# Layer-norm statistics of the last three pairs placed two rounds later, and the Silu table load placed behind the last softmax exponent

## The chip, the core and the metric

The kernel runs on one core of a Trainium2 chip. The core has five engines with an instruction stream each, executed in order: TensorE (PE in the profile; PEld is its weight load), VectorE (DVE), ScalarE (ACT), GpSimd (POOL) and SyncE (SP). They wait for each other and for DMA transfers through semaphores. SP and POOL each issue DMA transfers in this kernel. The metric is the device time of one execution in microseconds (us); lower is better. The time before is 755.1 us, the median of three runs (752.46, 755.1 and 756.65).

## The reference, cut to what matters

Input `x` is 32 sequences of 56 tokens with 256 features; `ctx` is 32 contexts of 1500 rows by 256 with a mask. There are four residual steps, each on a layer norm of what came before:

```python
x = x + xattn0(layernorm(x), ctx)          # decayed scan over the context, its mean projected, layer norm
x = x + ffn0(layernorm(x))                 # 16 experts, the best 6 of each token, hidden width 176
x = x + xattn1(layernorm(x), ctx, mask)    # softmax(q k / 16) over unmasked rows, times the rows
x = x + ffn1(layernorm(x))                 # 2 experts, the better one of each token, hidden width 1024
# an expert: (silu(h @ w_gate.T) * (h @ w_up.T)) @ w_down.T, weighted by its gate's softmax
```

`layernorm` subtracts the mean over the 256 features and divides by the root of the variance plus 1e-5. In `xattn1` queries are the rows of the norm, and keys and values are both the context rows. The mask leaves a run of rows at the end of each context, so the kernel reads a window of 384 rows per context (and has a branch at its end for inputs to which this doesn't apply; it is not taken here).

## The kernel before, in words

All arithmetic is in fp32. Two sequences together are a *pair*: 2 x 64 partitions, of which 2 x 56 hold tokens, so there are 16 pairs (`NP`), and the residual stream stays in SBUF as `xr[:, p, :]`, 128 partitions by 256 features for pair `p`.

There are four stages, each with its tile pools, so each begins as the one before ends:

1. The context scan (`xattn0`), the norm, the first gate and a sort of the tokens by expert.
2. The first expert stage: 99 blocks of 128 sorted rows. Each block's rows are gathered by POOL, multiplied with the weights of its expert, and its result is written to a DRAM buffer `ys0`. As blocks are done, the six results of each token are fetched again and added to `xr`. For pairs 0 to 12 (`NS` = 13) this is done inside the stage, by plain gathers and adds on DVE, and so are their statistics (mean and variance of `xr[:, p, :]`, function `stats_into`, lines 862 to 865: one bn_stats, one aggregate).
3. The attention (`xattn1`), lines 1107 to 1386.
4. The second expert stage (`expert_blocks` from line 1387 on): 15 blocks of four units, each unit gate and up products (L785), Silu on ACT (L791), a product on DVE (L795), two transposes (L803), a copy (L805) and the down product (L812). It begins with the rows that were sorted first.

In stages 2 to 4 a manual schedule is in force: every engine executes its instructions in the order in which the program text emits them. So the place of a line in the text is its place in the queue of its engine.

The attention is a loop over rounds `p` = 0 to 16 (line 1327). One round holds work of several pairs, one step apart:

- at `p == NR - 6` = 4 and `p == NP - 5` = 11, the roots of statistics that are ready (`roots_of`, lines 882 to 887: Ln and Exp on ACT, L189 and L190, then L885 on DVE); at round 11 those of pairs 13, 14, 15
- the normalised row block of pair `p + 2` (`query_rows`, ACT, L890), which reads these roots
- the root of pair `p - 2`'s last norm (ACT, L189 and L190)
- the scores of pair `p` (TensorE, L1133 and L1139) and the attended rows of pair `p - 1` (TensorE, L1174)
- the row maximum of pair `p` (DVE, L1147) and the softmax exponent (ACT, L1152)
- the last norm and gate of pair `p - 2` (DVE, L1200, L1207)
- attended rows times the softmax inverse plus residual, of pair `p - 1` (`sort_rows`, DVE, L1190), into a *payload* tile `pay`, and its statistics (L183, L184); then, in the round of pair 7's payload, the issue of the second expert stage's weights on SP (`load_w1`, L1101 and L1105)
- for pair `p + 2` the transposes of the query (TensorE L902, copied by ACT, L904) and of the window (TensorE L913, copied by DVE and ACT in turns, L916)
- the transposes of pair `p`'s probabilities (TensorE L1166, copied by ACT, L1167)
- for each four pairs the choice of expert, the rank and the place of each token (`sort_four`, `sort_rank`, `sort_place`), and four scatters of the payloads into sorted order by POOL (L1258)
- three of the 18 accumulating gathers of pairs 13 to 15 (`added`, POOL, L1318): each adds one of six results from `ys0` to `xr[:, p, :]` by DMA, so all stand in POOL's queue ahead of what the later rounds give it, and a pair's next gather waits for its last one. POOL runs behind the other engines here: it issues the last of them at 555.10 us, in the time of round 8
- at the end of round 8 (`p == NP - 8`), the statistics of pairs 13, 14 and 15 (`stats_into`, DVE, L864 and L865)
- in round 11 the order of the sorted blocks (`order_of_blocks`, one TensorE product, L1274, and ten DVE instructions from L1275 to L1291), in round 12 the first three gathers of sorted rows (L1305), and in round 15 the transposes and the copy of the first of them (L195, L197).

Round 16 holds only what is left of pairs 14 and 15.

Buffers matter in two places. The pool of payload tiles has nine buffers (line 1111), used in turn, so from pair 9 on a payload is written to a buffer that an earlier one's scatter must have left. And the PSUM pool `at_x` has four banks for the five transposes of a round (one of the query, four of the window), so the window's last transpose needs the bank that the query's copy (L904) empties. The attended rows have one PSUM bank: the next attend waits until DVE has read the one before (L1190).

ACT's functions come in table sets, one of which is active at a time. The attention opens with an explicit request for the set that holds Ln and Exp (L1121). The set for Silu is not asked for in the text: its load stands directly ahead of the first Silu of stage 4 (L791).

Of the kernel before, what the change touches and what calls it, by code (L numbers as in the profile page):

```python
# [22 lines left out]
NP = B // 2  # L23
# [35 lines left out]
def xattn_ffn_kernel(  # L59
# [23 lines left out]
    V, A, PE, G = nc.vector, nc.scalar, nc.tensor, nc.gpsimd  # L83
# [783 lines left out]
    def roots_by_steps(mv, n=1):  # L867

        m, v, y, r = (mv[..., i] if n > 1 else mv[:, i : i + 1] for i in range(4))
        i = y.bitcast(I32)  # L870
        yield lambda: V.tensor_scalar(v, v, EPS, None, ALU.add)  # L871
        yield lambda: V.tensor_scalar(i, v.bitcast(I32), 1, None, ALU.logical_shift_right)
        yield lambda: V.tensor_scalar(i, i, -1.0, float(0x5F3759DF), ALU.mult, ALU.add)
        c = small.tile([P, NP], F32, tag="nw", name="c")[:, 0:n]
        for _ in range(3):
            yield lambda: V.tensor_tensor(c, y, y, ALU.mult)
            yield lambda: V.tensor_tensor(c, c, v, ALU.mult)
            yield lambda: V.tensor_scalar(c, c, -0.5, 1.5, ALU.mult, ALU.add)
            yield lambda: V.tensor_tensor(y, y, c, ALU.mult)
        yield lambda: V.scalar_tensor_tensor(r, m, -1.0, y, ALU.mult, ALU.mult)  # L880

    def roots_of(a, b):

        inverse_root(mvq[:, a:b, 2], mvq[:, a:b, 1])
        V.scalar_tensor_tensor(  # L885
            mvq[:, a:b, 3], mvq[:, a:b, 0], -1.0, mvq[:, a:b, 2], ALU.mult, ALU.mult
        )
# [4 lines left out]
    def query_rows(p, pool):  # L892

        xn = pool.tile([P, D], F32, tag="xq_n", bufs=2, name="xn")
        normed(xn, xr[:, p, :], mvq[:, p])
        return xn

    def queries(p, pool, ps, tag, xn):

        tp = ps.tile([P, 512], F32, tag=tag, name="tp")  # L900
        for k in range(KD):
            PE.transpose(tp[:, k * P : (k + 1) * P], xn[:, k * P : (k + 1) * P], ident)  # L902
        xqs[p] = pool.tile([P, KD, P], F32, tag="xq", bufs=2, name="xq")
        A.activation(  # L904
            xqs[p].rearrange("p k c -> p (k c)"), tp[:, 0:D], AF.Copy, scale=ISC
        )
# [191 lines left out]
    def load_w1():  # L1098
        for m, w in ((0, wg1), (1, wu1)):
            for k in range(KD):  # L1100
                nc.sync.dma_start(  # L1101
                    out=w1_sb[:, :, (2 * k + m) * fq : (2 * k + m + 1) * fq],
                    in_=w[:, k, :].rearrange("p (e f) -> p e f", f=fq),
                )
        nc.sync.dma_start(  # L1105
            out=w1_sb[:, :, 2 * KD * fq : W1].rearrange("p e (c d) -> p e c d", d=D),
            in_=wd1.rearrange("p (e c) d -> p e c d", c=2),
        )
# [3 lines left out]
    with tc.manual_schedule(  # L1112
# [13 lines left out]
        def scores(p):  # L1126

            sps = psc.tile([P, 512], F32, tag="sp", name="sp")
            cT, xq = cTs.pop(p), xqs.pop(p)
            halves = [(h, slice(64 * h, 64 * h + 64)) for h in range(2)]  # L1130
            for h, r in halves:
                b = 2 * p + h
                PE.matmul(  # L1133
                    sps[r, 0:WIN], lhsT=pick[:, b : b + 1].to_broadcast([P, 64]),
                    rhs=terms.rearrange("b (q j) -> b j q", j=JW), start=True, stop=False,
                )
            for k in range(KD):
                for h, r in halves:
                    PE.matmul(  # L1139
                        sps[r, 0:WIN], lhsT=xq[:, k, r], rhs=cT[:, h, k, :],  # L1140
                        start=False, stop=(k == KD - 1),
                    )
            return sps

        def highest(sps):
            nb = small.tile([P, 4], F32, tag="nb", name="nb")
            V.tensor_reduce(nb[:, 0:1], sps[:, 0:WIN], AX.X, ALU.max, negate=True)  # L1147
            return nb

        def softmax(sps, nb):  # L1150
            sc = at.tile([P, WIN], F32, tag="sc", name="sc")
            A.activation(sc, sps[:, 0:WIN], AF.Exp, bias=nb[:, 0:1], accum_out=nb[:, 1:2])  # L1152
            return sc

        def inverse(nb):
            V.reciprocal(nb[:, 1:2], nb[:, 1:2])

            V.scalar_tensor_tensor(
                nb[:, 2:3], nb[:, 0:1], 0.5 * BIG, nb[:, 1:2], ALU.is_lt, ALU.mult
            )  # L1160
# [9 lines left out]
        def attend(p, pT):  # L1170
            op = po.tile([P, 512], F32, tag="op", name="op")
            for j in range(JW):
                for h in range(2):
                    PE.matmul(  # L1174
                        op[64 * h : 64 * h + 64, 0:D],
                        lhsT=pT[:, j, 64 * h : 64 * h + 64], rhs=window(p, h)[:, j, :],
                        start=(j == 0), stop=(j == JW - 1),
                    )
            return op
# [8 lines left out]
        def sort_rows(p, op, nb):  # L1188
            pay[p] = payp.tile([P, WP], F32, tag="pay", name="pay")
            V.scalar_tensor_tensor(  # L1190
                pay[p][:, D : 2 * D], op[:, 0:D], nb[:, 2:3], xr[:, p, :], ALU.mult, ALU.add
            )
            G.tensor_copy(pay[p][:, WP - 1 : WP], toks[:, p : p + 1])
            return stats(pay[p][:, D : 2 * D])

        def sort_root(mv):
            inverse_root(mv[:, 2:3], mv[:, 1:2])

        def sort_norm(p, mv):
            V.tensor_scalar(  # L1200
                pay[p][:, 0:D], pay[p][:, D : 2 * D], mv[:, 0:1], mv[:, 2:3],
                ALU.subtract, ALU.mult,
            )

        def sort_gate(p):
            gx = so.tile([P, D], F32, tag="gx", name="gx")
            V.scalar_tensor_tensor(  # L1207
                gx, pay[p][:, 0:D], 1.0, gd, ALU.mult, ALU.mult, accum_out=dd[:, p : p + 1]
            )
# [103 lines left out]
        def apart():  # L1313

            G.memset(gap, 0.0)
# [11 lines left out]
        for p in range(NP + 1):  # L1327
            if p == NR - 6:
                roots_of(NR, NS)
            if p == NP - 5:  # L1330
                roots_of(NS, NP)

            if p + 2 < NP:
                xn = query_rows(p + 2, at)
            if p - 2 in mvs:
                if p < NP:
                    sort_root(mvs[p - 2])
                else:
                    for step in roots_by_steps(mvs[p - 2]):
                        step()  # L1340
            if p < NP:
                sps = scores(p)
            if held:
                op = attend(held[0], held[1])
            if p < NP:
                nb = highest(sps)
                sc = softmax(sps, nb)
            if p - 2 in mvs:
                sort_norm(p - 2, mvs.pop(p - 2))
                sort_gate(p - 2)  # L1350
            if held:
                mvs[held[0]] = sort_rows(held[0], op, held[2])
                if held[0] == 7:
                    load_w1()
                held = None
            if p + 2 < NP:
                queries(p + 2, at, px, "x", xn)
                cTs[p + 2] = at.tile([P, 2, KD, WIN], F32, tag="cT", name="cT")
                for i in range(2 * KD):
                    turn(p + 2, i, px, "x", V.tensor_copy if i % 2 == 0 else A.copy)  # L1360
                    if i == 0:
                        inverse(nb)
            elif p < NP:
                inverse(nb)
            if p < NP:
                held = (p, turned(sc), nb)
            if four:
                sort_place(*four[0], sort_rank(four.pop()[1], ppt, "pt"))
            if 0 <= p - 2 and (p - 2) % GP == GP - 1:
                o = p - 2 - GP + 1  # L1370
                four.append((o, sort_four(o)))
            for q in range(NP - NS):
                if todo:
                    added(*todo.pop(0))
            if p == NP - 8:
                for q in range(NS, NP):
                    stats_into(mvq[:, q], xr[:, q, :])
            if p == 11:
                order_of_blocks()
            if p == 12:  # L1380
                for i in range(NY1):
                    apart()
                    rows_of1(i, payp, "pay")
            if p == NP - 1:
                xT1 = turned_rows(so, px, "x", xb1[0][:, 0:D])
# [229 lines left out]
```

## Time and profile before

The profiled execution took 789.92 us, and its span from first to last instruction is 788.0 us.

| stage | us from start | length | PE busy | DVE busy | ACT busy | granted PE clock | DMA share | GB/s |
|---|---|---|---|---|---|---|---|---|
| context scan, sort | 0 to 214 | 214.0 | 157.73 | 149.11 | 56.14 | 0.87 | 0.87 | 303 |
| first experts | 214 to 513 | 299.0 | 268.72 | 131.94 | 105.52 | 0.97 | 0.54 | 161 |
| attention | 513 to 602.42 | 89.42 | 80.53 | 62.68 | 50.90 | 0.96 | 0.72 | 209 |
| second experts | 602.42 to 788 | 185.58 | 172.99 | 60.86 | 29.69 | 0.99 | 0.11 | 34 |

All times are microseconds. "Busy" is the time in which an engine had an instruction in execution; matmuls are pipelined, so a busy TensorE isn't TensorE at its peak. The granted clock is a share of full speed. The DMA share is the mean busy share of the core's 16 DMA engines. In the timeline lines that follow, the first number is the start from the span's beginning, the second the time taken; then come engine, line of the kernel, operation, and the tile written and those read (`out<-in`), and in brackets the idle time of that engine just before the instruction with what ended it. The chain of waits is followed back from the last instruction: at each step to what released it, or to the instruction before it on its engine. What ended a wait is inferred from semaphore events.

### The profile page before, as it was taken

What the parts mean: (1) busy time and instruction counts of PE and PEld (TensorE: products, weight loads), DVE (VectorE), ACT (ScalarE), POOL (GpSimd) and SP (SyncE); (2) the same over time, 40 slices, a digit from 0 to 9 for tenths busy, and PEclk for the clock granted to TensorE, in tenths of its full rate; (3) what the DMA queues carried; (4) which work ended last, traced back from release to release, by engine and by line L of the source; (5) the groups of instructions that cost most, each with busy time, mean ns of one, the idle gap of its engine ahead of it and who ended that gap; (6) DMA issues with size and microseconds to landing.
All of it is one profiled execution on the core that took longest, in us unless ns stands there. A gap on an engine that the chain in (4) does not pass through costs nothing.

```text
span 788.0 us, 13691 instructions
## 1 busy us (share of the span) xinstructions
PE 680.0 (86%) x4147; PEld 447.8 (57%) x4147; DVE 404.6 (51%) x1386; ACT 242.2 (31%) x716; POOL 354.0 (45%) x444
## 2 busy tenths in 40 slices
PE   3477988887789889889899889899797999999995
PEld 3334545554467667556667566666464566666663
DVE  3568677788436436234444345667587333233321
ACT  0123233333134333333333333366463111111110
POOL 5355566643343465556656665457542411122110
PEclk9879799997699999899999999999899999999998
DMA  8969899999258976334434444387961200110100
GB/s 260 351 258 376 321 346 381 359 340 238 72 161 269 329 224 197 107 106 137 133 114 131 133 133 134 107 251 181 257 224 48 94 13 21 41 35 27 33 27 18
DMA packets 71426, 137.69 MB, mean 175 GB/s; under 512 B 7859, under 2 KB 43844, under 8 KB 71348
## 3 DMA queue, kind: packets, MB, share of 16 engines
q1 hardware_dynamic: 56612, 100.84, 37.4%
q0 software_dynamic: 14736, 35.90, 16.9%
q8 instruction: 39, 0.64, 0.3%
q14 instruction: 39, 0.32, 0.1%
HBM read 110.07 MB, written 27.29 MB: 174 GB/s over the span
## 4 chain that ended last, share of the span: by engine, by line
PE 72%; DVE 7%; DMA 5%; ACT 3%; issue 3%; POOL 3%; another core or an unknown queue 1%; POOLq 0%; ACTq 0%; DVEq 0%
PE gu L785 29%; PE y L812 18%; PE acc L325 6%; PE tp L803 4%; PE tp L195 4%; DMA xr<-ys,back 4%; ACT xT L197 2%; PE owned L593 1%; POOL xr L1318 1%; PE bp L467 1%; PE lp L505 1%; POOL xn L491 1%; PE sT L459 1%; PE tp L913 1%
## 5 line engine op out<-in xcount | busy, mean ns | idle before, releaser
L785 PE MATMUL gu<-w_sb,xT 128*128 x396 | 142.1, 482 | 23.9 <-ACT xT L197 19.7
L943 POOL DMA_INDIRECT xb<-xn,idx x99 | 96.6, 976 | 103.1 <-PE tp L195 52.1
L791 ACT ACTIVATE sg<-gu 128x176 f32<-128x176 f32 (+1 forms) x159 | 54.4, 342 | 239.5 <-PE gu L785 206.9
L797 DVE SCALAR_TENSOR_TENSOR hs<-sg,wgt,gu 128x176 f32<-128x176 f32 x99 | 39.3, 397 | 158.4 <-ACT sg L791 136.3
L785 PE MATMUL gu<-ring,xT 128*128 x240 | 112.9, 593 | 0.5 <-issue 0.5
L785 PEld LDWEIGHTS gu<-w_sb,xT 128*128 128x128 f32 x396 | 73.6, 194 | 61.9 <-ACT xT L197 27.5
L812 PE MATMUL y<-w_sb,hT 88*128 x396 | 103.6, 384 | 0.8 <-ACT yb L951 0.8
L856 POOL DMA_INDIRECT g<-ys,early x78 | 74.0, 949 | 33.5 <-issue 18.0
L795 DVE TENSOR_TENSOR hs<-sg,gu 128x256 f32<-128x256 f32 x60 | 25.2, 421 | 112.5 <-ACT sg L791 110.2
L803 PEld LDWEIGHTS tp<-ident,hs 128*88 128x88 f32 (+1 forms) x318 | 41.3, 131 | 61.4 <-issue 48.4
L812 PEld LDWEIGHTS y<-w_sb,hT 88*128 88x128 f32 x396 | 68.6, 193 | 7.1 <-ACT yb L951 1.0
L1423 POOL DMA_INDIRECT out<-ob,ti x15 | 14.9, 990 | 127.4 <-DVE ob L1420 127.1
L805 DVE COPY hT<-tp 88x256 f32<-88x256 f32 (+1 forms) x159 | 66.0, 415 | 3.8 <-PE y L812 2.8
L197 ACT COPY xT<-tp 128x256 f32<-128x256 f32 x130 | 48.4, 372 | 56.9 <-PE tp L195 39.3
L785 PEld LDWEIGHTS gu<-ring,xT 128*128 128x128 f32 x240 | 45.3, 190 | 33.0 <-issue 30.1
L803 PE MATMUL tp<-ident,hs 128*88 128x128 f32 (+1 forms) x318 | 61.6, 276 | 0.7 <-DVE mv L871 0.6
L812 PE MATMUL y<-ring,hT 128*128 x240 | 61.7, 380 | 0.0
L951 ACT COPY yb<-y 128x256 f32<-128x256 f32 x99 | 37.1, 375 | 61.2 <-PE y L812 31.0
L325 PE MATMUL acc<-ring,cz 128*32 128x256 f32 x768 | 54.9, 444 | 0.3 <-DVE cz L301 0.3
L195 PE MATMUL tp<-ident,xb 128*128 128x128 f32 x228 | 44.8, 279 | 2.4 <-issue 2.4
L432 POOL TENSOR_SCALAR z<-xr,mva,rsa 128x256 f32<-128x256 f32 x16 | 23.0, 1437 | 49.6 <-DVE xr L479 45.4
L812 PEld LDWEIGHTS y<-ring,hT 128*128 128x128 f32 x240 | 41.0, 190 | 3.3
(306 smaller groups left out, 1000.8 us busy)
## 6 DMA issues: line engine op xcount, KB each, us to landing
ring<-in_cx SPq DMA_DIRECT2D x32, 1536.0 KB
ys<-yb SPq DMA_DIRECT2D x99, 128.0 KB
ring<-in_cx SPq DMA_DIRECT2D x16, 384.0 KB
extra<-in_cx SPq DMA_DIRECT2D x16, 384.0 KB
xs<-zrow SPq DMA_DIRECT2D x5, 771.0 KB
w_sb<-in_wg SPq DMA_DIRECT2D x2, 1408.0 KB
w_sb<-in_wu SPq DMA_DIRECT2D x2, 1408.0 KB
xn<-xn SPq DMA_DIRECT2D x16, 128.0 KB
```

The lines of the kernel that those rows point to most:

```text
L195: PE.transpose(tp[:, k * P : (k + 1) * P], xn[:, k * P : (k + 1) * P], ident)
L197: A.copy(xT.rearrange("p k c -> p (k c)"), tp[:, 0 : KD * P])
L325: PE.matmul(acc[Q * g : Q * g + Q, 0:D], lhsT=cz[:, j, 1 - h : 1 - h + Q], rhs=c[:, j, :], start=(h == 0 and m == 0), stop=(h == 1 and m = ...
L785: PE.matmul(gu[:, 0 : 2 * fp], lhsT=xT[i][:, k, :], rhs=w[:, bass.ds(at[i] + (u * piece + k * 2 * fp), 2 * fp)], start=(k == 0), stop=(k = ...
L791: A.activation(sg, gu[:, 0:fp], AF.Silu)
L797: V.scalar_tensor_tensor(hs[i, u], sg, wgt[:, i : i + 1], up, ALU.mult, ALU.mult)
L803: PE.transpose(tp[0:h, c * P : (c + 1) * P], a[:, c * h : (c + 1) * h], ident)
L805: V.tensor_copy(hT[i, u], tp[0:h, 0 : 2 * P])
L812: PE.matmul(y[i][:, 0:D], lhsT=a[:, c * P : (c + 1) * P], rhs=w[0:h, bass.ds(at[i] + (u * piece + doff + c * D), D)], start=(u == 0 and c ...
L856: G.indirect_dma_start(out=g, out_offset=None, in_=ys0[0 : n * P, :], in_offset=bass.IndirectOffsetOnAxis(ap=at[:, p, k : k + 1], axis=0),)
L943: G.indirect_dma_start(out=xb, out_offset=None, in_=xn0, in_offset=bass.IndirectOffsetOnAxis(ap=idx[:, i : i + 1], axis=0),)
L951: A.copy(yb, y[:, 0:D])
```

## The change

Two places in the loop over rounds are edited. The statistics of pairs 13, 14 and 15 move from the end of round 8 to the end of round 10; their roots stay at the opening of round 11. And in round 15, directly behind the last softmax exponent, the set of functions that holds Silu is asked for; Tanh, which the second expert stage uses once (L1226), is run without a further load before and after. In the built order of instructions nothing else differs: the load that stood ahead of the first Silu stands behind the exponent of round 15, ahead of the copy of the probabilities (L1167) and of the first sorted rows (L197), and the six DVE instructions of the statistics stand 31 rows later in DVE's order, behind the placement of pairs 4 to 7 (L1247 to L1255) and ahead of L885.

```diff
             if p < NP:
                 nb = highest(sps)
                 sc = softmax(sps, nb)
+                if p == NP - 1:
+                    A.preload_act_table_set("silu_and_others")
             if p - 2 in mvs:
                 sort_norm(p - 2, mvs.pop(p - 2))
                 sort_gate(p - 2)
...
             for q in range(NP - NS):
                 if todo:
                     added(*todo.pop(0))
-            if p == NP - 8:
+            if p == NP - 6:
                 for q in range(NS, NP):
                     stats_into(mvq[:, q], xr[:, q, :])
```

## The prediction

> **What bounds the kernel now.** I read the page first for the chain of work that ended last, and then went into the attention stage, the only one that the diff touches.
>
> The page's chain, shares of the span by engine and line:
>
> ```profile
> PE 72%; DVE 7%; DMA 5%; ACT 3%; issue 3%; POOL 3%; another core or an unknown queue 1%; POOLq 0%; ACTq 0%; DVEq 0%
> ```
>
> TensorE carries most of it, but 4.0% of the span on that chain is one DMA, xr<-ys,back, the accumulating gathers of the last three pairs. They lie at 517 to 564 us. Where they end is in the DVE timeline of 557 to 565 us (start, duration, engine, line, and in brackets the idle time before and who ended it):
>
> ```profile
> 557.36 0.42 DVE L864 BATCH_NORM_STATS2 st<-xr 128x6 f32<-128x256 f32 x1
> 557.82 0.18 DVE L865 BATCH_NORM_AGGREGATE mvq<-st 128x2 f32<-128x6 f32 x1
> 559.52 0.43 DVE L864 BATCH_NORM_STATS2 st<-xr 128x6 f32<-128x256 f32 x1 [1.52 <-DMA xr<-ys,back]
> 559.98 0.18 DVE L865 BATCH_NORM_AGGREGATE mvq<-st 128x2 f32<-128x6 f32 x1
> 563.78 0.43 DVE L864 BATCH_NORM_STATS2 st<-xr 128x6 f32<-128x256 f32 x1 [3.61 <-DMA xr<-ys,back]
> 564.24 0.18 DVE L865 BATCH_NORM_AGGREGATE mvq<-st 128x2 f32<-128x6 f32 x1
> 564.34 0.52 DVE L1147 TENSOR_REDUCE nb<-sp 128x1 f32<-128x384 f32 x1
> ```
>
> These are the three statistics that the diff moves. DVE reaches them at the end of round 8 and stands for 1.52 + 3.61 = 5.13 us; only then does round 9's row maximum (L1147) run, and ACT's exponent and the query's copy wait behind that. TensorE's timeline of the same place:
>
> ```profile
> 556.97 0.44 PE L1133 MATMUL sp<-terms,pick 128*64 128x384 bf16 x2
> 557.24 1.46 PE L1139 MATMUL sp<-cT,xq 128*64 128x384 f32 x8
> 558.53 1.46 PE L1174 MATMUL op<-extra,pT 128*64 128x256 f32 x12
> ...
> 565.89 0.90 PE L913 MATMUL tp<-ident,extra 128*128 128x128 f32 x3 [4.55 <-ACT xq L904]
> 566.59 0.84 PE L1166 MATMUL tp<-ident,sc 128*128 128x128 f32 x3
> ```
>
> TensorE idles 4.55 us. Each round opens with L1133, so rounds are measured from one to the next. Before this they start at 526.86, 531.82, 536.78, 541.74 (round 6), 547.05, 552.01 and 556.97 (round 9): 4.96 us each, 5.31 in round 6, which holds a rank product. Then rounds 10, 11, 12, 13, 14 start at 567.36, 574.35, 579.42, 585.28, 590.24. Round 9 took 10.39 (5.43 too many); round 10, with a rank product like round 6, took 6.99 (1.68 too many). The second surplus is the clock. Busy time by stretch; the last three columns are granted clock, DMA share, GB/s:
>
> ```profile
> 561.35:565.85 4.50, 0.00 (x0) 0.00 (x0) 2.00 (x7) 0.95 (x4) 1.09 (x4) 0.81 1.08 365
> 565.00:570.00 5.00, 4.11 (x16) 2.30 (x18) 4.16 (x19) 3.25 (x10) 0.68 (x6) 0.50 1.06 283
> 598.70:600.40 1.70, 0.02 (x3) 0.04 (x2) 0.61 (x2) 0.58 (x2) 1.45 (x4) 1.00 0.48 186
> 600.40:605.00 4.60, 4.08 (x18) 2.13 (x19) 3.98 (x24) 0.54 (x1) 1.57 (x8) 1.00 0.28 104
> ```
>
> After 4.55 us of idleness the clock is half; after the 1.68 us at 598.7 it stays whole.
>
> The other edit concerns the table load ahead of the first Silu of the second expert stage; ACT's two lines and DVE's two:
>
> ```profile
> 604.46 1.28 ACT L791 ACT_TABLE_LOAD   x1 [5.18 <-PE gu L785]
> 605.75 0.76 ACT L791 ACTIVATE sg<-gu 128x256 f32<-128x256 f32 x2
> ...
> 605.82 0.18 DVE L184 BATCH_NORM_AGGREGATE mv<-st 128x2 f32<-128x6 f32 x1
> 606.17 0.42 DVE L795 TENSOR_TENSOR hs<-sg,gu 128x256 f32<-128x256 f32 x1 [0.16 <-ACT sg L791]
> ```
>
> The chain runs through this load, yet DVE waits only 0.16 us for what follows it: it is busy without a gap from 599.76 to 606.0.
>
> **What the Trainium skill says.** "TensorE: Matmul & The Clock Gate", Part 1, has the array's clock halved after an idle window of about 3.4 us, and whole again after as long a busy one; the two idle times above (4.55 halves, 1.68 doesn't) agree. "DMA: Bandwidth & Descriptors", Issuing engines are not separate DMA queues, says that transfers from all queues share the same 16 engines; here the last gather took 8.65 us from issue (555.10) to release (563.75) while the second expert stage's weights ran at 365 GB/s. "ScalarE: Activation LUTs", What ACT_TABLE_LOAD costs, gives 1283 ns plus about 1380 ns of drain; the trace has the 1.28 us and no drain: the Silu starts 0.01 us after it.
>
> **The change, part by part.** No instruction is added or dropped; the order built for the changed kernel differs only in where the three pairs of statistics and the table load stand.
>
> *Wait removed in round 9.* The gathers stand in rounds 0 to 5 of POOL's queue and the weights are issued in round 8, both ahead of the edit, so the last still lands at 563.8. Round 9 goes back to 4.96: −5.43.
>
> *Clock in round 10.* No idleness over 3.4 us is left there, so it takes 5.31: −1.68. Round 11 then starts at 556.97 + 4.96 + 5.31 = 567.24 instead of 574.35, 7.11 earlier.
>
> *New lateness in round 11.* Before, the statistics had two rounds of slack to their roots (L885, round 11); now they stand directly ahead. In round 7, which follows the same work as round 11, DVE is through with the placement (L1255) 1.23 us after the round's first matmul. Three statistics at a pitch of 0.56 (row 555.63 to 556.19: bn_stats 0.46, aggregate 0.10) end at 1.23 + 1.68 + 0.08 = 2.99. Then ACT's Ln and Exp, 0.35 + 0.24 (574.52 to 575.11), DVE's L885 0.20, and the query's row (L890) starts at 3.80; in the old round 11 it started at 575.31 − 574.35 = 0.96. Its 0.60 ends at 4.40, where TensorE, through with attend at 3.02, has idled 1.4 us (below both the 1.68 and the 3.4). ACT then does the second root until 4.82, the exponent (0.58), the query's copy to 5.68. Two transposes from 4.45, nine of the window's to 5.80, the last three, which need the copy's PSUM buffer, to 6.13, the probabilities' to 6.46. The old round 11 had this at 579.21 − 574.35 = 4.86. So +1.6. Round 12 waits on DVE's block order (L1275 to L1291) as before; DVE and TensorE come equally late to it, so nothing more. DVE's 0.95 us of idleness ahead of L1275 could take some back: bounds +0.6 and +2.0.
>
> *What else is late or early.* In round 10, pair 9's payload (L1190) takes the buffer of pair 0's, which must have been scattered. It comes at round 10 + 3.63 (as in round 6: 545.37 − 541.74) = 565.56. The scatters' bytes move at about 0.2 MB per us from 561.7 (POOL's queue in 1 us stretches: 0.21, 0.16, 0.24, 0.21, 0.11 MB from 562 on), 0.26 MB for each, and the gather before them was released 1.7 us after its bytes: pair 0's is free at about 565. No wait, but narrowly: 0 to +1.5. The second four scatters now fall into the weights' transfer, which ends some 2 us later, near 582; its weights are first used at about 597. That is hidden, as is the gather of the first sorted rows.
>
> *The table load.* It moves from 604.46 to behind the exponent of round 15 (597.22 + 0.66 = 597.88), so it ends at 599.16. The copy of the probabilities moves from 598.52 to 599.16 and that of the first rows to 599.54, ending 599.92. The attend of pair 15 isn't ready before 600.39: DVE's L1190 waits until 599.60 for a scatter. The first gate product comes at 602.42. So both delays lie under that scatter; without it, they would cost at most 0.64. The gain isn't 1.28 but what DVE waited, up to the end of its aggregate: about 0.2 (0 to 0.4). Of the load, 1.1 us was covered by DVE's chain of small steps.
>
> *Sum:* −5.43 − 1.68 + 1.6 − 0.2 = −5.7 us, bounds −6.9 (0.6, and 0.4 for the table) and −3.6 (2.0 and 1.5 for the scatter, 0 for the table). It is made against the profiled execution (789.92 us, span 788.0). The timed runs have a median of 755.1, so 34.8 us, 4.4%, aren't in them. The attention rounds are bound by TensorE at full clock and should take the same; the stall comes from DMA being late, which may differ. Carried over unscaled: 755.1 − 5.7 = 749.4.
>
> **Rivals.**
>
> *The stall is smaller in the timed runs.* If the missing 4.4% lies in DMA, the 48 us from first gather issued (515.8) to last landed (563.8) shrink by 2 to 5 us while rounds keep 4.96. With 3.2 us off, DVE waits about 2, TensorE's clock stays whole, and the removed surplus is 5.43 − 3.2 = 2.2: −2.2 + 1.6 − 0.2 = −0.8, so 754.3. For it: POOL itself waited 8.1 us on its gathers. Against: between 534 and 557 most gathers follow at POOL's own pitch, 1.54 + 0.30.
>
> *The wait moves.* Pair 9's payload waits for the scatter, or DVE finds the last gather unlanded in round 10 too: up to +2 of the gain back, 751.5. Against: 568.47 for the first statistic is 4.7 us after the landing.
>
> *Slower.* No stall in the timed runs (last gather landed before 558.5), while round 11's new idleness halves the clock. This needs idleness past a point between 1.68 and 4.55. The price is that of the cold pass from 565.89 to 572.06: 6.18 us for work that takes 3.65 warm, +2.5; with +1.6 − 0.2 that is +3.9: 759.0. Against: 1.4 us is short.
>
> *It does nothing:* excluded for placement by the built order; for time it is the first rival.
>
> **How the numbers follow.** A measurement of this kernel can tell about 0.5%, 3.8 us, from no change (three runs lie within 4.2). Forecast (749.4 ± 2) 0.46; smaller stall 0.36, a ninth of which passes 0.5% all the same; moved wait 0.10, half faster; slower 0.08. Faster: 0.45 + 0.04 + 0.05 = 0.54; same 0.01 + 0.32 + 0.05 = 0.38; slower 0.08. The likeliest's own range is 747.4 to 751.5; for 8 in 10 it must reach over the smaller stall with the run to run spread: 746.8 to 756.5.
>
> **What would show it.** In the profile after: L864 at the end of round 10, no bracket with xr<-ys,back; round 9 at 4.96 and 10 at 5.31; clock 1.00 from 560 to 575; round 11 near 6.7 with TensorE waiting 1.4 ahead of L902; the table load near 597.9 after the exponent and L795 waiting on nothing. Wrong would be: a bracket of a scatter on L1190 in round 10, a half clock in round 11, or a full gain in the profile and none in the times, which is the first rival.

## The result, and the profile after

The changed kernel takes 749.25 us (median of 20 runs, 744.4 to 752.75); the kernel before, run beside it, takes 753.94 us (median of 20, 752.04 to 756.65). The ratio is 0.9929, 95% interval 0.9915 to 0.9942: faster by 0.7%, clear of the 0.5% that the prediction took as the least that can be told from no change. The profiled execution took 748.76 us (span 746.9 us), which is in the middle of its timed runs, other than the first profiled execution of the kernel before (789.92). Nearly all of those 41 us lie elsewhere: from the first expert product to the first round of the attention it took 298.4 us there (214.08 to 512.45) and 260.2 us here (214.31 to 474.47), in a stretch whose program is the same in both. The experiments ran in several sittings too, in some of which the kernel before took near 753 us and in some 792 to 799. So ratios are given only against runs of the same sitting, and profiles are compared by rounds of the attention, counted from its own start.

The chain that ended last, by engine, from the page of the changed kernel:

```profile
PE 79%; DVE 9%; ACT 3%; POOL 2%; issue 2%; DMA 0%; POOLq 0%; DVEq 0%; ACTq 0%
```

The 5% of DMA are gone: no accumulating gather is on the chain any more. DVE's timeline at the end of round 10 and the opening of round 11:

```profile
530.25 0.16 DVE L1255 COPY cum<-cum 128x2 f32<-128x2 f32 x1
530.32 0.42 DVE L864 BATCH_NORM_STATS2 st<-xr 128x6 f32<-128x256 f32 x1
530.78 0.18 DVE L865 BATCH_NORM_AGGREGATE mvq<-st 128x2 f32<-128x6 f32 x1
530.88 0.40 DVE L864 BATCH_NORM_STATS2 st<-xr 128x6 f32<-128x256 f32 x1
...
531.84 0.18 DVE L865 BATCH_NORM_AGGREGATE mvq<-st 128x2 f32<-128x6 f32 x1
532.62 0.17 DVE L885 SCALAR_TENSOR_TENSOR mvq<-mvq 128x3 f32<-128x3 f32 x1 [0.61 <-ACT mvq L190]
532.71 0.55 DVE L1147 TENSOR_REDUCE nb<-sp 128x1 f32<-128x384 f32 x1
```

The statistics run straight through, none with a bracket. But now the roots come directly behind them: DVE waits 0.61 us for ACT's Ln and Exp before it can form L885. What that does to TensorE in rounds 11 and 12:

```profile
529.25 0.44 PE L1133 MATMUL sp<-terms,pick 128*64 128x384 bf16 x2
...
533.48 0.44 PE L902 MATMUL tp<-ident,xn 128*128 128x128 f32 x2 [1.20 <-ACT xn L890]
...
535.66 0.44 PE L1133 MATMUL sp<-terms,pick 128*64 128x384 bf16 x2
540.50 0.55 PE L913 MATMUL tp<-ident,extra 128*128 128x128 f32 x3 [0.47 <-ACT xq L904]
```

The idle time of 4.55 us in round 9 is gone; in its place TensorE idles 1.20 us in round 11, ahead of pair 13's query. By stretch (busy times; the last three columns are granted clock, DMA share, GB/s), rounds 10 and 11 run at full clock:

```profile
524.00:529.25 5.25, 5.25 (x44) 3.70 (x43) 4.67 (x21) 3.76 (x12) 0.74 (x6) 1.00 1.08 346
529.25:535.66 6.41, 5.21 (x43) 3.52 (x43) 4.90 (x21) 3.38 (x11) 3.91 (x7) 1.00 1.05 313
```

And the table load, in ACT's and DVE's timelines:

```profile
553.74 1.28 ACT L1349 ACT_TABLE_LOAD   x1
555.04 0.48 ACT L1167 COPY pT<-tp 128x384 f32<-128x384 f32 x1
...
560.41 0.39 ACT L791 ACTIVATE sg<-gu 128x256 f32<-128x256 f32 x1 [4.62 <-PE gu L785]
561.70 0.18 DVE L184 BATCH_NORM_AGGREGATE mv<-st 128x2 f32<-128x6 f32 x1
561.79 0.39 DVE L795 TENSOR_TENSOR hs<-sg,gu 128x256 f32<-128x256 f32 x1
```

The load stands behind the last exponent; the first Silu (560.41) is done a whole microsecond before DVE comes to L795, which has no bracket: it stands only behind DVE's own instructions.

Rounds of the attention in every profile (us from one L1133 to the next):

| kernel | round 9 | 10 | 11 | 12 | sum |
|---|---|---|---|---|---|
| before, first profile | 10.39 | 6.99 | 5.07 | 5.86 | 28.31 |
| changed | 4.96 | 5.30 | 6.41 | 5.64 | 22.31 |
| before, again | 9.50 | 7.21 | 5.08 | 6.63 | 28.42 |
| changed, again | 4.96 | 5.30 | 6.83 | 5.65 | 22.74 |
| statistics alone | 4.96 | 6.48 | 6.77 | 5.69 | 23.90 |
| table load alone | 10.21 | 6.95 | 5.08 | 6.68 | 28.92 |
| TensorE kept busy | 9.56 | 5.71 | 5.07 | 5.93 | 26.27 |
| one round earlier | 5.38 | 7.14 | 5.08 | 5.81 | 23.41 |
| weights held back | 6.49 | 5.31 | 5.07 | 6.79 | 23.66 |
| 11 payload buffers | 4.96 | 5.78 | 6.78 | 5.65 | 23.17 |
| the same, load not moved | 4.96 | 5.88 | 6.78 | 5.65 | 23.27 |
| statistics divided, 11 buffers | 4.96 | 5.31 | 5.16 | 5.74 | 21.17 |
| the same, a copy on ACT | 4.96 | 5.31 | 5.15 | 5.66 | 21.08 |
| the same, second stage filled | 5.58 | 5.41 | 5.52 | 7.89 | 24.40 |

### The profile page after: what moved, and what is told of

Its sections match the earlier page's. It is cut to its first block, busy times and chain, and to the rows that moved or that the text cites. A ratio compares the mean times of both kernels' runs of the same rounds, so it can differ in the third digit from the quotient of the medians.

```text
span 746.9 us, 13692 instructions
## 1 busy us (share of the span) xinstructions
PE 667.8 (89%) x4147; PEld 446.5 (60%) x4147; DVE 403.7 (54%) x1386; ACT 245.8 (33%) x716; POOL 352.5 (47%) x444
## 4 chain that ended last, share of the span: by engine, by line
PE 79%; DVE 9%; ACT 3%; POOL 2%; issue 2%; DMA 0%; POOLq 0%; DVEq 0%; ACTq 0%
PE gu L785 30%; PE y L812 18%; PE acc L325 7%; PE tp L803 5%; PE tp L195 4%; PE tp L913 2%; PE sp L1139 2%; PE op L1174 2%; PE owned L593 2%; PE bp L467 1%; PE lp L505 1%; POOL xn L491 1%; PE sT L459 1%; DVE st L183 1%; ACT xT L197 1%
## 5 line engine op out<-in xcount | busy, mean ns | idle before, releaser
L785 PE MATMUL gu<-w_sb,xT 128*128 x396 | 136.6, 467 | 3.4 <-ACT xT L197 2.0
L943 POOL DMA_INDIRECT xb<-xn,idx x99 | 94.8, 957 | 68.4 <-PE tp L195 41.6
L785 PE MATMUL gu<-ring,xT 128*128 x240 | 114.7, 601 | 0.6 <-issue 0.6
L812 PE MATMUL y<-w_sb,hT 88*128 x396 | 102.0, 379 | 0.0
L785 PEld LDWEIGHTS gu<-w_sb,xT 128*128 128x128 f32 x396 | 74.4, 191 | 32.2 <-ACT xT L197 3.6
L795 DVE TENSOR_TENSOR hs<-sg,gu 128x256 f32<-128x256 f32 x60 | 25.2, 420 | 113.9 <-ACT sg L791 113.9
L785 PEld LDWEIGHTS gu<-ring,xT 128*128 128x128 f32 x240 | 45.8, 192 | 33.6 <-issue 30.8
L197 ACT COPY xT<-tp 128x256 f32<-128x256 f32 x130 | 48.5, 373 | 44.4 <-PE tp L195 43.4
```

Of the source, the lines that this page charges most:

```text
L197: A.copy(xT.rearrange("p k c -> p (k c)"), tp[:, 0 : KD * P])
L785: PE.matmul(gu[:, 0 : 2 * fp], lhsT=xT[i][:, k, :], rhs=w[:, bass.ds(at[i] + (u * piece + k * 2 * fp), 2 * fp)], start=(k == 0), stop=(k = ...
L812: PE.matmul(y[i][:, 0:D], lhsT=a[:, c * P : (c + 1) * P], rhs=w[0:h, bass.ds(at[i] + (u * piece + doff + c * D), D)], start=(u == 0 and c ...
L943: G.indirect_dma_start(out=xb, out_offset=None, in_=xn0, in_offset=bass.IndirectOffsetOnAxis(ap=idx[:, i : i + 1], axis=0),)
```

## The experiments

The theory to be tested is the prediction's: a wait of DVE on the last gathers, in every execution; a clock that falls behind it; a smaller lateness in round 11 in exchange; and a table load that was hidden. Its main rivals: the stall belongs to the long execution that was profiled first; the clock costs nothing of its own; the load was worth its 1.28 us. Each ratio below is to the kernel before in the same sitting, with its 95% interval in parentheses. Each profile is of one execution.

**The kernel before, a second time** (no edit).

> The kernel before, unchanged, for a second profile of it, since its first profiled execution (789.92 us) lay 36 us above the median of its runs. Theory (the stall belongs to every execution): the third statistic of pair 15 waits for its gather at the end of round 8, DVE stands 4 to 6 us in sum, round 9 takes 10 to 11 us and round 10 about 7 at a clock of a half, although the span is near 752. Rival (the stall is a thing of the long execution): waits under 2 us and round 9 under 7.

Measured: 800.81 us in a sitting where the kernel before has a median of 799.34. The last statistic in DVE's timeline:

```profile
573.53 0.43 DVE L864 BATCH_NORM_STATS2 st<-xr 128x6 f32<-128x256 f32 x1 [4.19 <-DMA xr<-ys,back]
```

The wait is 4.19 us, rounds 9 and 10 are 9.50 and 7.21. The theory's stall is there again, and it is there in the two further profiles below that keep the statistics in round 8 and the weights where they were (4.95 and 4.97 us). But all four are of executions of 789 to 801 us, so they don't settle the rival: no profile shows the kernel before in an execution near 753. What speaks for the stall there is the profile of the changed kernel, at 748.76 us. Each of these gathers shows as 144 packets on POOL's DMA queue (queue 0). That queue moved none from the start of round 9 (518.99) to 521.4, and 98 up to 523.99, 5.0 us into the round, so the last gather hadn't landed by then either. Without a wait DVE would have come to its statistic about 1.5 us into round 9 (557.87 after 556.39 in the kernel with the weights held back, below).

**The statistics alone** (edit against the changed kernel).

```diff
                 sc = softmax(sps, nb)
-                if p == NP - 1:
-                    A.preload_act_table_set("silu_and_others")
             if p - 2 in mvs:
```

> The change's first edit alone: statistics at the end of round 10, table load where it was. Theory: -5.5 us, so a ratio to before of 0.9927, and the change itself not to be told from it. Rival (the table load is worth its whole 1.28 us): -4.1, 0.9946.

Measured: 0.9957 (0.9933 to 0.9981). That is less of a gain than expected, whose 0.9927 lies just outside the interval, and by time it stands closer to the rival. But in its profile from pair 14's payload (L1190, 597.03) to the first product of the second stage (L795, 603.50) it takes 6.47 us, as in the kernel before (599.76 to 606.17, 6.41), where the changed kernel takes 6.19 (555.60 to 561.79). So the load is worth about 0.3 us here, and most of what the profile lacks lies in round 10 (6.48 instead of 5.30): ACT's window copy waits there 1.71 us for transposes that by TensorE's timeline had ended. The last section comes back to that.

**The table load alone** (edit against the changed kernel).

```diff
-            if p == NP - 6:
+            if p == NP - 8:
                 for q in range(NS, NP):
                     stats_into(mvq[:, q], xr[:, q, :])
```

> The change's second edit alone: statistics at the end of round 8, the table for Silu asked for behind the last exponent. Theory: -0.2 us, 0.9997, not to be told from no change; in the profile from DVE's last payload wait (L1190 of pair 14) to its first expert product (L795) 6.2 us instead of 6.4. Rival: -1.28 us, 0.9983.

Measured: 0.9974 (0.9943 to 1.0005), an interval that holds both values. The profile decides: from L1190 (604.24) to L795 (610.46) it takes 6.22 us, and L795 has no bracket. The load moved is worth 0.2 us. All profiles with nine payload buffers agree: with the load where it was, the same stretch takes 6.28 to 6.50 us (five profiles), with the load moved 6.14 to 6.22 (four).

**TensorE kept busy through the stall** (edit against the kernel before).

```diff
                 for i in range(2 * KD):
+                    if p == 9 and i == 3:
+                        for _ in range(5):
+                            d = ppt.tile([P, 512], F32, tag="pt", name="d")
+                            PE.matmul(
+                                d, lhsT=ident, rhs=xr[:, 0:2, :].rearrange("p j d -> p (j d)"),
+                                start=True, stop=True,
+                            )
                     turn(p + 2, i, px, "x", V.tensor_copy if i % 2 == 0 else A.copy)
```

> The kernel before with five more products of 128 by 512 (results unread) in round 9 ahead of the window's last transpose, where TensorE stood idle; the stall itself stays. Theory (part of the loss is the clock): TensorE's clock stays 1.00, round 10 takes 5.31 instead of 6.99 and the transposes after the stall take their full-clock time, -2.5 us in sum if the products (about 0.9 us each) end inside the stall; -1.5 to -2.5, 0.997 to 0.998. Rival (the clock costs nothing that other waits don't cover): 1.000 or above.

Measured: 0.9982 (0.9956 to 1.0008), as expected in size but not told from nothing by time. TensorE's timeline and the stretches:

```profile
570.77 4.46 PE L1363 MATMUL d<-xr,ident 128*128 128x512 f32 x10
575.32 0.55 PE L913 MATMUL tp<-ident,extra 128*128 128x128 f32 x3
```

```profile
571.00:575.00 4.00, 4.00 (x10) 1.52 (x8) 1.73 (x7) 0.68 (x3) 1.19 (x4) 1.00 1.06 361
575.00:580.00 5.00, 4.91 (x37) 3.00 (x37) 4.42 (x21) 2.91 (x9) 0.67 (x6) 1.00 1.06 294
```

DVE's waits are those of the table-load kernel (2.09 + 2.88 = 4.97 us against 1.89 + 3.06 = 4.95), the clock is 1.00 in both stretches, and rounds 9 and 10 take 15.27 us against 17.16. So, by these two profiles, 1.9 us of the loss was the clock; the expectation had 1.5 to 2.5.

**One round earlier** (edit against the changed kernel).

```diff
-            if p == NP - 6:
+            if p == NP - 7:
                 for q in range(NS, NP):
                     stats_into(mvq[:, q], xr[:, q, :])
```

> The changed kernel with the statistics one round earlier, at the end of round 9 rather than 10. Theory (the last gather lands about 51.5 us after round 0 began, and DVE is through with round 9 at about 51.6): almost no wait on the gathers; the 1.68 us of statistics then make round 10 late by 1 to 1.7 and round 11 falls back to about 5.1; the same time as the change within 0.2%. Rival (the gather lands later in most executions): DVE waits 1 to 3 us and half of the gain is lost, ratio to before 0.995 to 0.998.

Measured: 0.9931 (0.9904 to 0.9957), next to the change's own 0.9929. No statistic waits on a gather; round 10 is late by 1.83 us (7.14 instead of 5.31), round 11 back at 5.08. The theory holds; the lateness goes where the statistics go.

**The weights held back** (edit against the kernel before).

```diff
-                if held[0] == 7:
+                if held[0] == 9:
+                    nc.sync.dma_start(out=xn0[0:P, 0:1], in_=pay[9][:, D : D + 1])
                     load_w1()
```

> The kernel before (statistics in round 8) with the second expert stage's weights held back on SP by a store of one column of pair 9's payload (512 bytes, into a buffer no longer read), so that they start in round 10. Theory (the weights share the DMA engines with the last gathers, but the gathers' own pace of about 2.4 us each makes most of the lateness): the last gather takes about 7.2 us instead of 8.65, DVE waits about 3.7 instead of 5.1 in sum, TensorE idles about 3 us, the clock may stay whole; -1.4 to -4 us, 0.995 to 0.998. Rival (the weights make the stall): wait under 1.5 us, -6 to -7, 0.991.

Measured: 0.9954 (0.9933 to 0.9975). POOL's issue of the last gather, in the kernel before and here, and DVE's timeline at the end of round 8 here:

```profile
555.10 1.54 POOL L1318 DMA_INDIRECT xr<-ys,back  x1 [0.30 <-issue]
```

```profile
553.95 1.56 POOL L1318 DMA_INDIRECT xr<-ys,back  x1 [0.30 <-issue]
```

```profile
557.34 0.40 DVE L864 BATCH_NORM_STATS2 st<-xr 128x6 f32<-128x256 f32 x1
557.77 0.18 DVE L865 BATCH_NORM_AGGREGATE mvq<-st 128x2 f32<-128x6 f32 x1
557.87 0.39 DVE L864 BATCH_NORM_STATS2 st<-xr 128x6 f32<-128x256 f32 x1
558.30 0.18 DVE L865 BATCH_NORM_AGGREGATE mvq<-st 128x2 f32<-128x6 f32 x1
558.40 0.53 DVE L1147 TENSOR_REDUCE nb<-sp 128x1 f32<-128x384 f32 x1
```

No wait at all: the last gather landed in less than 557.87 − 553.95 = 3.9 us, where beside the weights it took 8.65 (8.4 to 9.1 in the three other profiles with a stall). My theory of the gathers' own pace is wrong; the rival is right that the weights' transfer makes the stall. The time isn't the rival's −6 to −7 us but −3.6, since rounds 9 and 12 have other losses here (6.49 and 6.79, the first with a 1.23 us wait of DVE's L1190 on TensorE). The weights were still moving at 586 to 591 us (373 GB/s).

**Eleven payload buffers, with and without the early load** (edit against the changed kernel; the second takes the early load out again).

```diff
-    payp = ctx.enter_context(tc.tile_pool(name="pay", bufs=9))
+    payp = ctx.enter_context(tc.tile_pool(name="pay", bufs=11))
```

> The changed kernel with 11 payload buffers instead of 9, so that pairs 14 and 15 don't wait for the scatters of pairs 8 and 9. Theory: DVE's wait of 1.79 us ahead of pair 14's payload goes and its chain of small steps into the second expert stage starts that much earlier; the attend of pair 15 is then bound by the copy of the probabilities behind the table load (at most 0.64 us); -1.2 to -1.8 us against the change, ratio to before about 0.991. Rival (something else holds the second expert stage, the scatters or the first rows): no difference from the change, 0.993.

Measured: 0.9892 (0.9849 to 0.9934). Pair 14's payload, which in the changed kernel waits for a scatter,

```profile
555.60 0.48 DVE L1190 SCALAR_TENSOR_TENSOR pay<-op,nb,xr 128x256 f32<-128x256 f32 x1 [1.79 <-DMA xs<-pay,to]
```

doesn't wait any more (597.95 below, no bracket), and from the start of round 15 (594.81) to L795 (604.20) it takes 9.39 us, against 11.11 in the changed kernel (550.68 to 561.79): −1.72, as expected. The six timed runs alone don't show that it beats the change, since the interval holds 0.9929.

> The same with 11 payload buffers, without the early request for the Silu table (the load stands ahead of the first Silu again). Theory (the load is hidden in the kernel before by DVE's lateness, and that lateness is now 1.8 us less): the load costs more here than the 0.2 us that it cost before, 0.5 to 1.0 us above the one with the request; in the profile L795 waits for ACT's Silu 0.5 us or more. Rival: as before, 0.2.

Measured: 0.9922 (0.989 to 0.9955). DVE's timeline, first of the kernel with the early load, then of the one without:

```profile
597.95 0.48 DVE L1190 SCALAR_TENSOR_TENSOR pay<-op,nb,xr 128x256 f32<-128x256 f32 x1
...
604.20 0.39 DVE L795 TENSOR_TENSOR hs<-sg,gu 128x256 f32<-128x256 f32 x1
```

```profile
593.44 0.48 DVE L1190 SCALAR_TENSOR_TENSOR pay<-op,nb,xr 128x256 f32<-128x256 f32 x1
...
600.37 0.42 DVE L795 TENSOR_TENSOR hs<-sg,gu 128x256 f32<-128x256 f32 x1 [0.63 <-ACT sg L791]
```

6.25 us against 6.93: with DVE no longer late, the load where it was costs 0.68 us, three times as much as in the kernel before. It was hidden by DVE's lateness, as the theory has it. The two times alone, whose intervals overlap, don't tell it.

**The changed kernel again, and the statistics divided.** No edit in the first; in the second, on top of the eleven buffers:

```diff
             if p == NP - 5:
-                roots_of(NS, NP)
+                roots_of(NS, NS + 1)
...
-            if p == NP - 6:
-                for q in range(NS, NP):
+            if p == NP - 8:
+                stats_into(mvq[:, NS], xr[:, NS, :])
+            if p == NP - 6:
+                for q in range(NS + 1, NP):
                     stats_into(mvq[:, q], xr[:, q, :])
+            if p == NP - 5:
+                roots_of(NS + 1, NP)
             if p == 11:
```

> The changed kernel, unchanged, on the chip of the experiments, which runs all of this slower (about 795 us before), as the mark for the two that follow. Theory: 0.992 to 0.995 of before, as measured first (0.9929); no wait on the gathers in round 10, round 11 near 6.5 us and rounds 11 and 12 together near 12.2, against 11 to 11.8 in the kernel before.

Measured: 0.9925 (0.9904 to 0.9946), in a sitting where the kernel before takes 753.58 us and not the 795 that the expectation names. Rounds 11 and 12 take 12.48 us together.

> The changed kernel with 11 payload buffers, and the statistics divided: pair 13's in round 8 (its gather had landed there in all four profiles with the statistics in round 8), pairs 14 and 15 in round 10, and the roots of 14 and 15 at the end of round 11 ahead of the block order instead of at its opening. Theory (round 11 is late because three statistics and three roots stand ahead of pair 13's query on DVE and ACT): TensorE doesn't wait ahead of L902 in round 11, which takes 5.0 to 5.4 us, round 12 up to 6.2; -0.5 to -1.4 us against 11 buffers alone, so about 0.988 of before. Rival (DVE's sum of work over rounds 9 to 12 is what counts, wherever it stands): rounds 9 to 12 shorter only by the 0.56 us of one statistic.

Measured in the same sitting: 0.9906 (0.9885 to 0.9927), 745.92 us against 748.44 for the changed kernel. TensorE and DVE at round 11:

```profile
532.89 1.46 PE L1174 MATMUL op<-extra,pT 128*64 128x256 f32 x12
534.31 0.44 PE L902 MATMUL tp<-ident,xn 128*128 128x128 f32 x2
```

```profile
533.49 0.13 DVE L885 SCALAR_TENSOR_TENSOR mvq<-mvq 128x1 f32<-128x1 f32 x1
...
537.75 0.15 DVE L885 SCALAR_TENSOR_TENSOR mvq<-mvq 128x2 f32<-128x2 f32 x1
```

The query's transposes follow the attend without a bracket; round 11 takes 5.16. Rounds 9 to 12 are 1.57 us shorter than in the changed kernel of this sitting, more than the 0.56 us of one statistic. The buffers aren't what does it: with eleven buffers alone round 11 takes 6.78. So round 11's lateness was the chain of three statistics and their roots, not DVE's sum of work.

**One more window copy on ACT.**

```diff
-                    turn(p + 2, i, px, "x", V.tensor_copy if i % 2 == 0 else A.copy)
+                    turn(p + 2, i, px, "x", V.tensor_copy if i == 0 or i == 2 and p != 11 else A.copy)
```

> The same with one more of round 11's window copies (the third, 0.47 us on DVE) on ACT instead of DVE. Theory (DVE's work sets rounds 11 and 12, ACT has 2 us to spare there): round 12 comes down by 0.3 to 0.5 us, TensorE waits 0.2 us or less ahead of its last three window transposes; about 0.9875 of before, not to be told from the last one by its time. Rival (ACT is then late with the probabilities): round 12 opens later by 0.4.

Measured: 0.9901 (0.9879 to 0.9922), 746.21 us. Round 12 comes down by 0.08 us only, and TensorE still waits 0.48. That is neither the theory's 0.3 to 0.5 nor the rival's lateness.

**The second expert stage filled.** (Why is told in the last section.)

```diff
             if t == 2:
+                for _ in range(2):
+                    d = ptr.tile([P, 512], F32, tag="tr", name="d")
+                    PE.matmul(
+                        d, lhsT=ident, rhs=xr[:, 0:2, :].rearrange("p j d -> p (j d)"),
+                        start=True, stop=True,
+                    )
                 sort_place(*four[0], sort_rank(four.pop()[1], ptr, "tr"))
```

> The kernel with divided statistics, 11 buffers and the window copy on ACT, and two products of 128 by 512 (results unread, about 0.9 us each) on TensorE at the start of the second expert stage, where it stands idle 1.88 us ahead of the last rank product (L1235). Theory (in the profile of the changed kernel and in seven other profiles, but not in the profiles of the kernel before, this idleness is followed by a spell of half clock that costs up to 3.3 us, and it depends on how the idleness falls): the clock stays 1.00 from 5 to 15 us after the first expert product, the second expert stage takes about 181.8 us from its first L795 to the end; 0.986 to 0.989 of before. Rival (the spell comes from elsewhere or the added products push the rank): clock under 1 there again, or L1235 later, 0.990 or above.

Measured: 0.9917 (0.9882 to 0.9951), in a sitting at 797 us. In its profile the clock is 1.00 from 605.36 to 620.36 us and the stage takes 181.84 us from the first L795, as the theory said; but round 12 took 7.89 us in this execution, and by its time the version isn't shown to be better than the one before it. Which version is the fastest stays open: eleven buffers alone have 0.9892, the divided statistics with eleven buffers 0.990 to 0.991, and all these intervals overlap each other and that of the change. That the divided statistics beat the change rests on the rounds of the profiles and on medians 2.5 us apart in one sitting.

## Why the prediction was right

The time was forecast as 749.4 us and is 749.25. That it was met so closely is in part luck: the forecast took 5.7 us from a base of 755.1, while the kernel before takes 753.94 beside the change and the medians differ by 4.7. The mechanism is borne out, and the size lies within its bounds of 3.6 and 6.9. Its steps, one by one:

- *Wait removed in round 9*, −5.43: 4.96 us in the profile, as said. That the stall isn't peculiar to one execution is shown by the second profile of the kernel before and by two more. That it is as large in the timed runs near 753 us, which the first rival doubted, is inferred and not shown by a profile: in the changed kernel's profile at 748.76 us the last gather hadn't landed 5.0 us into round 9 either, and the medians near 753 us differ by 4.7 and, in the second sitting at this level, by 5.1 us (753.58 and 748.44), where that rival had 0.8.
- *Clock in round 10*, −1.68: 5.30 us instead of 6.99, at clock 1.00. That the clock was a cost of its own is shown by the profile with the products in the stall, 1.9 us over rounds 9 and 10.
- *New lateness in round 11*, +1.6: 6.41 against 5.07, +1.34, with TensorE idle 1.20 us ahead of L902 (1.4 forecast); in the second profile of the change 6.83, +1.76, idle 1.63. Dividing the statistics took it away.
- *Round 12*, nothing: 5.64 after 5.86, −0.22. DVE's idleness ahead of the block order took a little back, which the bounds had foreseen.
- *Payload against scatter in round 10*, nothing: DVE's L1190 of pair 9 has no bracket. The weights were hidden too: the second stage's first product has only a 0.61 us issue gap.
- *Table load*, −0.2: −0.22 by the profile. The cover that was named (DVE's chain behind a scatter) was the right one, since the load's price rose to 0.68 when that chain began earlier.

From the start of round 9 to L795 the profile lost 49.20 − 42.80 = 6.40 us; 5.7 had been forecast, and the medians moved by 4.7 (by the ratio, 0.0071 of 753.94, 5.4). The forecast has no term for the second expert stage, where the profile of the changed kernel gives 3.3 us back (last section). How often that happens in the timed runs isn't known.

Three pieces of the reasoning were wrong without harm. I took the 34.8 us between the first profile and the timed runs for something that might shrink the stall; nearly all of it lies in the first expert stage. Against the smaller stall I argued from POOL's issue pitch; what made the last gather late was the weights' transfer, to which the 8.65 us beside 365 GB/s had pointed. With 3.9 us instead of 8.65 the third statistic would have waited half a microsecond at most. And I put the idle time after which the clock falls between 1.68 and 4.55 us; in the second expert stage idle times of 1.88 and 0.61 us, close together, were followed by a clock of 0.62. One reading was off by 0.16 us and changes nothing: the wait of pair 14's payload (L1190) ends at 599.76 and not at 599.60.

## What to carry to other kernels

An engine that executes in order pays for a waiting instruction with everything behind it: move the consumer of a late transfer to just ahead of its own consumer, but count what then stands back to back (here three statistics, two ACT functions and one DVE step, 1.3 to 1.8 us), and divide it if part of the data is there earlier. An instruction on the chain that ended last is worth only what the next engine waited for it: here 0.2 of 1.28 us, and 0.7 once DVE no longer came late. A stall that idles TensorE for microseconds has a second price behind it, in the clock.

## What was not expected of the hardware

**A half clock after short idle times, not in every execution.** Early in the second expert stage TensorE waits twice for DVE's sort. The kernel before, then the changed kernel:

```profile
611.99 0.39 PE L1235 MATMUL rk<-s,before 128*128 128x8 f32 x2 [1.88 <-DVE w L1225]
612.99 0.39 PE L1239 MATMUL rk<-cum,ones 128*128 128x8 f32 x2 [0.61 <-DVE cum L1229]
613.23 1.96 PE L785 MATMUL gu<-ring,xT 128*128 x4
```

```profile
567.58 0.39 PE L1235 MATMUL rk<-s,before 128*128 128x8 f32 x2 [1.88 <-DVE s L1216]
568.58 0.60 PE L1239 MATMUL rk<-cum,ones 128*128 128x8 f32 x2 [0.61 <-DVE cum L1229]
569.03 3.76 PE L785 MATMUL gu<-ring,xT 128*128 x4
```

The idle times are the same, 1.88 and 0.61 us, and the four products behind them (L785) take 1.96 us in one and 3.76 in the other. By stretch, the changed kernel's clock there:

```profile
566.79:571.79 5.00, 3.60 (x8) 1.96 (x9) 2.23 (x14) 0.21 (x1) 1.52 (x5) 0.62 0.00 0
571.79:576.79 5.00, 5.00 (x14) 2.51 (x13) 1.53 (x5) 0.38 (x1) 2.91 (x3) 0.70 0.42 163
```

The stage from the first L795 to the end took 181.83 us before and 185.11 after. A clock under 1 in this place shows in eight profiles (the changed kernel twice, statistics alone, TensorE kept busy, weights held back, eleven buffers without the early load, divided statistics twice) and not in five (the kernel before twice, table load alone, one round earlier, eleven buffers), with stages of 183.3 to 185.1 against 181.7 to 182.1 us. So keeping each idle time under the 3.4 us of the prediction was not enough. Of the eight profiles with the statistics moved six have the spell, of the five with the statistics in round 8 two; whether the change makes it more frequent is open. "TensorE: Matmul & The Clock Gate" in the Trainium skill, Part 1, says that the activity window of about 3.4 us runs freely. If so, whether two idle times with a short product between them make a window idle enough could depend on where it begins. What is seen doesn't contradict this: TensorE works 0.91 us in 565.2 to 568.6 and in 609.6 to 613.0 alike, and the filled stage stayed at full clock in its one profile. That the place of the window is the cause was not tested, and the five without the spell may have it in other executions. It may be a reason why single executions of one kernel differ by up to 3 us here.

**A wait on TensorE that TensorE's timeline doesn't show.** In six profiles ACT or DVE waits, in round 9 or 10, 0.7 to 2.0 us for TensorE work that by the timeline was done (statistics alone, one round earlier, weights held back, eleven buffers with and without the early load, second stage filled). These are the six profiles without a stall that took 786 to 789 us; the four without a stall that took 745 to 750 us (changed twice, divided statistics twice) have no such wait. So it seems to belong to the longer executions, of which more below. A transfer on the instruction queue (queue 8, one packet of 0.02 MB) lies near each of these waits, but every profile here has such a transfer in the first 5 us of round 9, with the wait or without. Whether TensorE stood for want of instructions is open, and so is whether the timeline is right there, since the ends of matmuls are modelled and some of their records can be missing; nothing was run to tell these apart.

**The sittings.** With the same program, the stretch from the first expert product to the attention took 298.4, 307.7 (before), 260.2 and 260.6 us (changed), while the 214 us ahead of it were alike within 1 us. The changed kernel's edits lie behind it. In the two longer ones TensorE waits there 19.7 and 23.2 us in sum for ACT's copies of the gathered rows (L785 on L197), in the two shorter ones 2.0 and 2.1 us. It isn't a property of one chip, as the expectation for the changed kernel's second profile had it: on the same chip (number 14 of the record) the kernel before took 792.17 us in one sitting and 753.58 in the next. What makes the difference is open.
